# A two-layer gated cross-attention block on one NeuronCore: the softmax sums of half the heads of layer 1 move to ScalarE

## The chip, the core and the metric

The kernel runs on one core of one Trainium2 chip. A core has TensorE (matmuls, transposes), VectorE, ScalarE, GpSimd and SyncE, each with its own queue that it works off in order; they wait for each other by semaphores. The metric is the device time of one execution in microseconds; before the change it is 2202.97 us, the median of three runs (2202.91 to 2205.18).

## What is computed

The reference is a decoder block of two layers for 8 samples. Each layer adds a cross-attention over a context and a feed-forward net to x, both behind a tanh gate. Cut to what matters here (layer 1 is the `L0` part):

```python
x = x + tanh(g_xattn[0]) * L0_xattn(layernorm(x), ctx, ctx, Wq, Wk, Wv, Wo)   # 16 heads of 32
x = x + tanh(g_ffn[0])   * L0_ffn(layernorm(x), w1, conv_w, conv_b, w2)       # ternary weights, depthwise conv
x = x + tanh(g_xattn[1]) * L1_xattn(layernorm(x), ctx, mask, Wq, Wkv, Wo)     # 8 heads of 64, mask
x = x + tanh(g_ffn[1])   * L1_ffn(layernorm(x), w_gate, w_up, w_down)         # blockwise fp4
# L0_xattn, per sample and head:
scores = q @ k.T / sqrt(32)                 # 224 x 750
attn = softmax(scores, axis=-1)
out = (attn @ v) ... @ Wo.T
```

x is 8 x 224 x 512, the context 8 x 750 x 512, all in float32.

## The kernel before

The program is unrolled. One loop in `run` goes over 16 attentions: n = 0 to 7 are the samples of layer 1 (`attention16`), 8 to 15 those of layer 2 (`attention8`); afterwards `ffn1` does the second feed-forward net. Other work is cut into small pieces, Python generators that yield an estimate of the TensorE time and the VectorE time of the piece. The attention routines put such pieces between their own instructions: `fill(us, queues)` takes pieces until their TensorE time reaches `us`, `pace(us, beside)` takes pieces until VectorE is thought to be `us` behind, and `finish` takes all. The order that results stands in each engine's queue.

For a sample n of layer 1 the pieces are: `early` (the output projections of sample n - 1, L383; the second product of the feed-forward net of sample n - 2, L929; the values of sample n, L359), `late` (`keys_queries` of sample n + 1: keys L298, queries L327, transposes of the normed x, L185) and `beside` (`ffn0` of sample n - 1: the product with w1, L822, then hp L830 on VectorE, y L834 on ScalarE, the taps L846 on VectorE, tanh L876 on ScalarE, the gate L858; in sample 0 the ternary quantization of both feed-forward weights, L715 to L731). What a product leaves in PSUM is copied out by ScalarE: kT (L307), v (L368), xnT and xqT (L186), bc (L204). These copies share two banks, tag `m`, and one bank, tag `t`.

`attention16` has two halves. The 512 columns are 4 groups g of 4 heads; queries are in 2 tiles of 112, keys in 2 chunks of 375 for the scores and in 6 tiles of 125 for the weights.

- Maxima: 16 slots (g, i, c). Four score matmuls (L466), one for each head, write a PSUM tile `quad` of four banks; VectorE takes the maximum over the chunk for all four heads (L473). Then comes fill. The maxima of all groups are joined (L485), split into three bf16 parts, and transposed.
- Weights: 12 steps, three for each group. For two key tiles TensorE puts minus the maximum (L434, bf16) and then the transposed scores (L443) into `quad`; ScalarE takes the exponential of all four heads at once (L510); fill and pace follow; then the products of the weights with v and with ones (both L521) add up in the bank `pa`, for which each head uses 32 columns of the array. The products with ones give the softmax sum in all 32 rows of the head. After the third step VectorE takes the reciprocal of the sums (L530) and multiplies (L531).

`quad` is allocated once (bufs=1): the next scores or weights wait until VectorE or ScalarE is done with it.

At the end of layer 2 the first two blocks of the last feed-forward net are already begun (`ffn1_head`); the hidden values of block 0 are quantized (`quantized`, in pieces of 512 columns and three parts) before `ffn1` starts, and `ffn1` then works block by block (L1076, L1108), with the load of w_down (`wd`) at its start.

## Time and profile before

| what | before |
|---|---|
| median of three runs | 2202.97 us |
| the profiled execution | 2205.97 us, span 2204.2 us |
| TensorE busy | 2139.1 us (97%) |
| VectorE busy | 1390.8 us (63%) |
| ScalarE busy | 698.1 us (32%) |
| samples 0 to 7 of layer 1 | 31.6 to 1018.4 us |
| one of them (sample 4) | 124.58 us, of which the maxima to the first weights 59.8 |
| products with v, L521 | 1536 records, 93.3 us |
| products with ones, L521 | 1536 records, 91.0 us |

The span is from the first to the last instruction of the profiled execution. A float32 matmul has two records in the trace. Matmuls on different rows or columns of the array run at once, so the busy time of such a group is far below its count times the mean of one.

### The profile page before, as it was taken

To read this page: it belongs to the slowest core of one execution; us is meant where nothing else is said; L and a number is where in the kernel's file an instruction comes from. 1 tells how busy PE (TensorE), PEld (TensorE's weight loads), DVE (VectorE), ACT (ScalarE), POOL (GpSimd) and SP (SyncE) were. 2 spreads that over 40 slices of the span, in tenths; PEclk is the share of its full clock that TensorE was granted. 3 is DMA by queue.
4 is the path that set the end of the run, shared out by engine and by line. 5 is a ranking of instruction groups with operands and counts; after the bars stand their busy time and mean duration, and the time that the engine had idled before them with its cause. 6 is when DMAs were issued, how large, how long until landed. Compare 5 with 4: busy or idle time off the path is not lost.

```text
span 2204.2 us, 33275 instructions
## 1 busy us (share of the span) xinstructions
PE 2139.1 (97%) x14094; PEld 1239.6 (56%) x14094; DVE 1390.8 (63%) x2611; ACT 698.1 (32%) x1180; POOL 131.4 (6%) x145
## 2 busy tenths in 40 slices
PE   9999999999999999999999999999999998999999
PEld 5544536455554646455555665656656565655555
DVE  3786777676776777675366485755523357666665
ACT  1222415152432515152443353443434231111111
POOL 0000000000000000000000110101100001111111
PEclk9999999999999999999999999999999999999999
DMA  6210010100001010211002112022210011000000
GB/s 221 72 34 29 1 45 2 32 15 18 29 12 35 2 45 2 70 34 37 29 19 66 51 49 64 28 71 57 60 38 11 14 40 51 10 19 19 20 5 20
DMA packets 50213, 81.31 MB, mean 37 GB/s; under 512 B 3344, under 2 KB 29712, under 8 KB 49936
## 3 DMA queue, kind: packets, MB, share of 16 engines
q1 hardware_dynamic: 50064, 79.18, 11.4%
q8 instruction: 111, 1.82, 0.3%
q14 instruction: 38, 0.31, 0.0%
HBM read 65.28 MB, written 13.89 MB: 36 GB/s over the span
## 4 chain that ended last, share of the span: by engine, by line
PE 86%; DVE 10%; ACT 2%; issue 1%; DMA 1%; SPq 0%; POOL 0%; ACTq 0%; DVEq 0%; POOLq 0%
PE ps_m L359 16%; PE ps_m L298 11%; PE ps_big L1076 10%; PE ps_m L1108 6%; PE ps_pa L521 6%; PE ps_quad L466 5%; PE ps_m L383 5%; PE ps_m L327 4%; PE ps_half L618 4%; PE ps_half L678 4%; PE ps_pa L581 3%; PE ps_quad L443 3%; PE ps_t L822 2%; PE ps_m L1076 2%; PE ps_t L929 1%; PE ps_quad L434 1%
## 5 line engine op out<-in xcount | busy, mean ns | idle before, releaser
L298 PE MATMUL ps_m<-cx,wk 128*128 128x375 f32 x1024 | 364.4, 488 | 2.4 <-ACT kT L307 1.2
L359 PE MATMUL ps_m<-wv,cx 128*125 128x512 f32 x768 | 355.2, 603 | 0.0
L473 DVE TENSOR_REDUCE part<-ps_quad 112x4 f32<-112x1500 f32 x128 | 220.1, 1720 | 125.3 <-PE ps_quad L466 125.2
L298 PEld LDWEIGHTS ps_m<-cx,wk 128*128 128x128 f32 x1024 | 181.7, 191 | 104.0 <-issue 20.2
L359 PEld LDWEIGHTS ps_m<-wv,cx 128*125 128x125 f32 x768 | 136.0, 187 | 174.6 <-issue 162.7
L510 ACT ACTIVATE p<-ps_quad 125x1792 f32<-125x1792 f32 x96 | 159.8, 1664 | 204.1 <-PE ps_quad L443 204.1
L635 DVE CUSTOM_DVE_ANT_0 ps_half<-ps_half,mbias 112x750 f32<-112x750 f32 x128 | 121.1, 946 | 163.4 <-PE ps_half L618 162.9
L368 ACT COPY v<-ps_m 125x512 f32<-125x512 f32 x96 | 56.3, 586 | 487.4 <-PE ps_m L359 486.9
L1108 PE MATMUL ps_m<-wd,hqT 128*128 128x512 f32 x308 | 136.6, 592 | 0.0
L656 ACT ACTIVATE p<-ps_half,nm 112x750 f32<-112x750 f32 x128 | 113.3, 890 | 57.8 <-DVE nm L647 57.5
L383 PE MATMUL ps_m<-wo,aT 128*112 128x512 f32 x256 | 120.8, 602 | 1.1 <-DVE worth L758 1.1
L466 PE MATMUL ps_quad<-kT,qT 32*112 32x375 f32 x1024 | 115.2, 519 | 6.0 <-DVE part L473 6.0
L846 DVE SCALAR_TENSOR_TENSOR y<-hp,cw,y 128x224 f32<-128x224 f32 x256 | 109.6, 449 | 4.5
L1076 PE MATMUL ps_big<-wg,xqT 128*128 128x352 f32 x352 | 111.3, 459 | 0.0
L1076 PE MATMUL ps_big<-wu,xqT 128*128 128x352 f32 x352 | 111.3, 459 | 0.0
L327 PE MATMUL ps_m<-xnT,wq 128*128 128x224 f32 x512 | 109.7, 361 | 0.6 <-ACT xnT L186 0.6
L521 PE MATMUL ps_pa<-p,v 125*32 125x224 f32 x1536 | 93.3, 361 | 14.8 <-ACT p L510 14.8
L678 PEld LDWEIGHTS ps_half<-ident,p 112*125 112x125 f32 x768 | 93.2, 188 | 19.1 <-issue 7.6
L683 ACT COPY p<-ps_half 125x672 f32<-125x672 f32 x128 | 86.3, 723 | 43.4 <-PE ps_half L678 42.3
L327 PEld LDWEIGHTS ps_m<-xnT,wq 128*128 128x128 f32 x512 | 94.9, 192 | 8.9 <-issue 4.2
L678 PE MATMUL ps_half<-ident,p 112*125 112x112 f32 x768 | 95.8, 273 | 2.5 <-ACT p L656 2.5
L618 PE MATMUL ps_half<-kT,qT 64*112 64x375 f32 x512 | 97.5, 498 | 0.0
(207 smaller groups left out, 2829.0 us busy)
## 6 DMA issues: line engine op xcount, KB each, us to landing
cx<-in_ctx SPq DMA_DIRECT2D x32, 750.0 KB, 4.3
wst<-in_w SPq DMA_DIRECT2D x16, 512.0 KB, 8.2
x<-in_x SPq DMA_DIRECT2D x8, 448.0 KB, 6.2
mid<-x SPq DMA_DIRECT2D x8, 448.0 KB, 3.1
x<-mid SPq DMA_DIRECT2D x8, 448.0 KB, 3.6
last<-x SPq DMA_DIRECT2D x8, 448.0 KB, 3.1
out<-yout SPq DMA_DIRECT2D x14, 256.0 KB, 2.0
wraw<-in_w_gate SPq DMA_DIRECT2D x11, 256.0 KB, 2.7
```

The source lines that it names most:

```text
L298: nc.tensor.matmul(pk, lhsT=self.w["wk"][:, k, g * 128 : (g + 1) * 128], rhs=job["cx"][c][:, k, :], start=k == 0, stop=k == KC - 1,)
L327: nc.tensor.matmul(pq[:, g - g0, :], lhsT=self.w["wq"][:, k, g * 128 : (g + 1) * 128], rhs=xnT[:, k, :], start=k == 0, stop=k == KC - 1,)
L359: nc.tensor.matmul(pv, lhsT=job["cx"][c][:, k, at : at + CP], rhs=self.w["wv"][:, k, :], start=k == 0, stop=k == KC - 1,)
L383: nc.tensor.matmul(po, lhsT=aT[:, g, i * TP : (i + 1) * TP], rhs=self.w["wo"][:, g, :], start=g == 0, stop=g == KC - 1,)
L466: nc.tensor.matmul(sc[:, h, :MH], lhsT=qT[r, g, i * TP : (i + 1) * TP], rhs=kT[g][r, c * MH : (c + 1) * MH], start=True, stop=True,)
L473: nc.vector.tensor_reduce(part[:, i, g, :, c], sc[:, :, :MH], AX.X, ALU.max)
L510: nc.scalar.activation(p, pw[:, :, : 2 * S], AF.Exp)
L521: nc.tensor.matmul(pa[r, which, :], lhsT=self.ones[:CP, r] if which else job["v"][j][:, col : col + 32], rhs=p[:, h, (j - j0) * S : (j - j ...
L618: nc.tensor.matmul(sc[h][:, c, :MH], lhsT=qT[r, g, i * TP : (i + 1) * TP], rhs=kT[g][r, c * MH : (c + 1) * MH], start=True, stop=True,)
L678: nc.tensor.transpose(pt[:, j // half, j % half * TP : (j % half + 1) * TP], p[:, h, j * CP : (j + 1) * CP], self.ident[:TP, :TP],)
L1076: nc.tensor.matmul(ps[:, :CW], lhsT=xqT[:, k, :], rhs=wt[:, k, c0 : c0 + CW], start=k == 0, stop=k == KC - 1,)
L1108: nc.tensor.matmul(po, lhsT=hqT[:, k, :], rhs=wd[:, k, :], start=k == 0, stop=k == NC1 - 1)
```

## The change

1. In the maxima half the scores go into two PSUM tiles `pair` of two heads (two banks each, bufs=2) in place of one `quad`, with one reduction for each; the maxima are kept negated. The weights use the same two tiles, with one exponential for each.
2. For groups 2 and 3, ScalarE also takes the exponential of the scores in the maxima half, with the negated maximum of the chunk as its bias, and adds it up (`accum_out`): 32 instructions of 112 x 375 a sample. What is written is not used; only the sums are. `divisors` later scales them by exp(chunk maximum - maximum), adds the two chunks, takes the reciprocal, and spreads it over the 32 rows of each head by two transposes and two bf16 products (`stat_inv`, `spread_q`).
3. The products with ones are made for groups 0 and 1 only.
4. The products of a step come behind the next step's scores, and those of the last step behind the first scores of the next sample (`rest`).
5. The times of `fill` and `pace` change: 2.0 in the slots of groups 0 and 1, about 3.9 in those of groups 2 and 3, where `beside` pieces are taken as well; 1.2 or 2.0 in the weights.
6. The transposes of the queries use a bank `m` from sample 1 on (before: from sample 10), and the pieces of the queries come in the middle of a key group.
7. What is left of the quantization of block 0's hidden values goes into `ffn1` (`left`).

The diff, cut to its core:

```diff
@@ queries, keys_queries
-            self.transposed(xnT, xn, i, "m" if n > B + 1 else "t")
+            self.transposed(xnT, xn, i, "m" if n else "t")
...
-                yield from self.keys(n, c, g)
-                if (c, g) in ((0, 0), (0, 1), (0, 3), (1, 0), (1, 1)):
-                    yield next(q)
+                for k, cost in enumerate(self.keys(n, c, g)):
+                    yield cost
+                    if k == 1 and (c, g) in ((0, 0), (0, 1), (0, 3), (1, 0), (1, 1)):
+                        yield next(q)
@@ attention16, maxima
-                    sc = self.ps("quad", [TP, 4, 512])
+                    sc = [self.ps("pair", [TP, 2, 512]) for _ in range(2)]
...
-                    nc.vector.tensor_reduce(part[:, i, g, :, c], sc[:, :, :MH], AX.X, ALU.max)
+                    for k in range(2):
+                        nc.vector.tensor_reduce(
+                            part[:, c, i, g, 2 * k : 2 * k + 2],
+                            sc[k][:, :, :MH], AX.X, ALU.max, negate=True,
+                        )
+                    if (g, i, c) == (0, 0, 0):
+                        self.finish([before])
                     self.behind = 0
...
+                    if g < 2:
+                        self.fill(3.4 if n and (g, i, c) == (0, 0, 0) else 2.0, early, late)
+                        continue
...
+                    for h in range(4):
+                        nc.scalar.activation(
+                            shown[:TP, h, :MH],
+                            sc[h // 2][:, h % 2, :MH],
+                            AF.Exp,
+                            bias=part[:, c, i, g, h : h + 1],
+                            accum_out=sums[:, c, i, g - 2, h : h + 1],
+                        )
+                    if (g, i, c) == (KC - 1, NT - 1, 1):
+                        self.fill(3.9, early, late)
+                        continue
+                    self.pace(0.1, beside)
+                    self.fill(1.9, early, late)
+                    self.pace(0.1, beside)
+                    self.fill(2.0 + max(self.behind - 2.4, 0), early, late)
...
-        self.fill(3.3, early, late)
+        self.pace(0.1, beside)
+        self.fill(2.9, early, late)
@@ attention16, weights
+        def divisors():
+            less = pool.tile([TP, 2, NT, 2, 4], F32, name="less")
+            for c in range(2):
+                nc.vector.tensor_tensor(
+                    less[:, c], val[:, :, 2:4, :], part[:, c, :, 2:4, :], ALU.subtract
+                )
+            nc.scalar.activation(less, less, AF.Exp)
+            yield
+            nc.vector.tensor_tensor(sums, sums, less, ALU.mult)
+            total = pool.tile([TP, NT, 2, 4], F32, name="total0")
+            nc.vector.tensor_tensor(total, sums[:, 0], sums[:, 1], ALU.add)
+            nc.vector.reciprocal(total, total)
+            transposed = self.stat_rows(self.stat_inv, total.rearrange("p t g h -> p t h g"))
...
+            iT = transposed()
...
+            nc.scalar.copy(across, pi)
+            yield across
...
+        def products(g, j0, p):
...
+            for which in range(2 if g < 2 else 1):
...
+        for step in range(KC * NKT // 2):
+            g, j0 = divmod(2 * step, NKT)
+            pw = [self.ps("pair", [CP, 2, 512]) for _ in range(2)]
...
+            for k in range(2):
+                nc.scalar.activation(p[:, 2 * k : 2 * k + 2, :], pw[k][:, :, : 2 * S], AF.Exp)
+            self.behind = max(self.behind - 4.1, 0)
+            if last:
+                products(*last)
+            last = g, j0, p
+            if step in (1, 3, 4, 5):
+                banks["across"] = next(more)
...
+            self.pace(3.0, beside)
+            self.fill(1.2 if g < 2 else 2.0, late)
@@ ffn1, run
+        first = left(h[0])
...
+                if i in (2, 3, 7, 8, 11, 13, 16, 18, 19):
+                    next(first, None)
...
-        self.psum_pool(banks, quad=1)
+        self.psum_pool(banks, pair=2)
...
-        self.finish(beside)
+        while beside and self.head["ready"] is None:
+            self.piece([beside])
         self.finish([rest, self.project_out(2 * B - 1)])
```

More of the change, by code (lines that the diff above doesn't have):

```diff
@@ L107, in setup @@
         self.spread_r = c.tile([128, 2, 128], BF16, name="spread")
+        self.spread_q = c.tile([128, 2, 128], BF16, name="spread_q")
         for g in range(KC):
@@ L112, in setup @@
             nc.vector.tensor_copy(self.pick[:, g, :], one.to_broadcast([128, CP]))
+            if g < 2:
+                own = c.tile([128, 4], F32, name="own4", bufs=2)
+                nc.vector.tensor_reduce(own, rows[:, :, 3 * g : 3 * g + 3], AX.X, ALU.add)
+                nc.vector.tensor_copy(
+                    self.spread_q[:, g, :].rearrange("p (h r) -> p h r", h=4),
+                    own.unsqueeze(2).to_broadcast([128, 4, 32]),
+                )
         for k in range(2):
@@ L124, in setup @@
         ]
-        for st in self.stat[0] + self.stat[1]:
+        self.stat_inv = c.tile([TP, NT, 128], BF16, name="stat_inv")
+        for st in self.stat[0] + self.stat[1] + [self.stat_inv]:
             nc.gpsimd.memset(st, 0.0)
@@ L449, in weights_minus_max, with attention16 @@
                 )
-    def attention16(self, n, early, late, beside):
+    def attention16(self, n, before, early, late, beside):
         nc, pool, job = self.nc, self.att, self.jobs[n]
@@ L457, in attention16 @@
         rows = [slice(h * 32, (h + 1) * 32) for h in range(4)]
-        part = pool.tile([TP, NT, KC, 4, 2], F32, name="part")
+        part = pool.tile([TP, 2, NT, KC, 4], F32, name="part")
+        sums = pool.tile([TP, 2, NT, 2, 4], F32, name="sums")
         for g in range(KC):
@@ L463, in attention16 @@
                 for c in range(2):
-                    sc = self.ps("quad", [TP, 4, 512])
+                    sc = [self.ps("pair", [TP, 2, 512]) for _ in range(2)]
                     for h, r in enumerate(rows):
                         nc.tensor.matmul(
-                            sc[:, h, :MH],
+                            sc[h // 2][:, h % 2, :MH],
                             lhsT=qT[r, g, i * TP : (i + 1) * TP],
@@ L472, in attention16 @@
                         )
-                    nc.vector.tensor_reduce(part[:, i, g, :, c], sc[:, :, :MH], AX.X, ALU.max)
-                    self.behind = 0
-                    if n and g > 1 and (i, c) in ((0, 1), (1, 1)):
-                        self.pace(0.1, beside)
-                        self.fill(3.7 if self.behind > 0.5 else 1.72, early, late)
-                    else:
-                        self.fill(2.9 if n and (g, i, c) == (0, 0, 0) else 1.72, early, late)
-                        if self.behind > 0.5:
-                            self.fill(0.86, early)
@@ L484, in attention16 @@
-        val = pool.tile([TP, NT, KC, 4], F32, name="val")
-        nc.vector.tensor_reduce(
-            val.rearrange("p t g h -> p (t g h)"),
-            part.rearrange("p t g h c -> p (t g h) c"),
-            AX.X,
-            ALU.max,
-            negate=True,
-        )
+                    for k in range(2):
+                        nc.vector.tensor_reduce(
+                            part[:, c, i, g, 2 * k : 2 * k + 2],
+                            sc[k][:, :, :MH],
+                            AX.X,
+                            ALU.max,
+                            negate=True,
+                        )
@@ new lines, in attention16 @@
+                    if (g, i, c) == (0, 0, 0):
+                        self.finish([before])
+                    self.behind = 0
+                    if g < 2:
+                        self.fill(3.4 if n and (g, i, c) == (0, 0, 0) else 2.0, early, late)
+                        continue
+                    if (g, i, c) == (2, 0, 0):
+                        shown = pool.tile([CP, 4, 2 * S], F32, name="p", bufs=2)
+                    for h in range(4):
+                        nc.scalar.activation(
+                            shown[:TP, h, :MH],
+                            sc[h // 2][:, h % 2, :MH],
+                            AF.Exp,
+                            bias=part[:, c, i, g, h : h + 1],
+                            accum_out=sums[:, c, i, g - 2, h : h + 1],
+                        )
@@ L492, in attention16 @@
+                    if (g, i, c) == (KC - 1, NT - 1, 1):
[5 more added lines that the diff above has]
+                    self.fill(2.0 + max(self.behind - 2.4, 0), early, late)
+        val = pool.tile([TP, NT, KC, 4], F32, name="val")
+        nc.vector.tensor_tensor(val, part[:, 0], part[:, 1], ALU.min)
         transposed = self.stat_rows(self.stat[0][n % 2], val.rearrange("p t g h -> p t h g"))
-        self.fill(3.3, early, late)
+        self.pace(0.1, beside)
@@ L496, in attention16 @@
         self.fill(0.7, late)
-        self.behind = 0
-        aT = job["aT"] = pool.tile([128, KC, S], F32, name="aT")
-        for g in range(KC):
-            pa = self.ps("pa", [128, 2, S])
-            for j0 in range(0, NKT, 2):
-                pw = self.ps("quad", [CP, 4, 512])
-                k = kT[g][:, j0 * CP : (j0 + 2) * CP]
-                self.weights_minus_max(
-                    [(pw[:, h, : 2 * S], r, g, qT[:, g, :], k) for h, r in enumerate(rows)],
-                    self.pick, sT, True,
-                )
-                p = pool.tile([CP, 4, 2 * S], F32, name="p", bufs=2)
-                nc.scalar.activation(p, pw[:, :, : 2 * S], AF.Exp)
-                self.behind = max(self.behind - 5.8, 0)
-                self.pace(1.5, beside)
-                self.fill(2.05 - self.ahead(4.0 if j0 + 2 < NKT else 0.5, beside), late)
-                self.pace(4.0 if j0 + 2 < NKT else 0.5, beside)
-                self.owed = 0
-                for which in range(2):
-                    for j in (j0, j0 + 1):
-                        for h, r in enumerate(rows):
-                            col = g * 128 + h * 32
-                            nc.tensor.matmul(
-                                pa[r, which, :],
-                                lhsT=self.ones[:CP, r] if which else job["v"][j][:, col : col + 32],
-                                rhs=p[:, h, (j - j0) * S : (j - j0 + 1) * S],
-                                start=j == 0 and which == 0,
-                                stop=j == NKT - 1 and which == 1,
-                            )
-            inv = pool.tile([128, 2, S], F32, name="inv")
-            nc.vector.reciprocal(inv[:, 0, :], pa[:, 1, :])
-            nc.vector.tensor_tensor(aT[:, g, :], pa[:, 0, :], inv[:, 0, :], ALU.mult)
-            self.behind += 2.0
@@ new lines, in attention16 @@
+        self.behind = max(self.behind - 3.0, 0)
+        def divisors():
[3 more added lines that the diff above has]
+                    less[:, c], val[:, :, 2:4, :], part[:, c, :, 2:4, :], ALU.subtract
+                )
+            nc.scalar.activation(less, less, AF.Exp)
[5 more added lines that the diff above has]
+            transposed = self.stat_rows(self.stat_inv, total.rearrange("p t g h -> p t h g"))
+            self.behind += 2.0
+            yield
+            iT = transposed()
+            yield
+            pi = self.ps("t", [128, 2, S])
+            for k in range(2):
+                nc.tensor.matmul(
+                    pi[:, k, :], lhsT=self.spread_q[:, k, :], rhs=iT, start=True, stop=True
+                )
+            across = pool.tile([128, 2, S], F32, name="inv")
+            nc.scalar.copy(across, pi)
+            yield across
@@ new lines, in attention16 @@
+        aT = job["aT"] = pool.tile([128, KC, S], F32, name="aT")
+        more, banks = divisors(), {}
+        def products(g, j0, p):
+            if j0 == 0:
+                banks["pa"] = self.ps("pa", [128, 2, S])
+            pa = banks["pa"]
+            for which in range(2 if g < 2 else 1):
+                for j in (j0, j0 + 1):
+                    for h, r in enumerate(rows):
+                        col = g * 128 + h * 32
+                        nc.tensor.matmul(
+                            pa[r, which, :],
+                            lhsT=self.ones[:CP, r] if which else job["v"][j][:, col : col + 32],
+                            rhs=p[:, h, (j - j0) * S : (j - j0 + 1) * S],
+                            start=j == 0 and which == 0,
+                            stop=j == NKT - 1 and (which == 1 or g > 1),
+                        )
+            if j0 + 2 < NKT:
+                return
+            if g < 2:
+                inv = pool.tile([128, S], F32, name="inv16")
+                nc.vector.reciprocal(inv, pa[:, 1, :])
+                self.behind += 2.0
+            else:
+                inv = banks["across"][:, g - 2, :]
+                self.behind += 0.4
+            nc.vector.tensor_tensor(aT[:, g, :], pa[:, 0, :], inv, ALU.mult)
@@ new lines, in attention16 @@
+        last = None
+        for step in range(KC * NKT // 2):
+            g, j0 = divmod(2 * step, NKT)
+            pw = [self.ps("pair", [CP, 2, 512]) for _ in range(2)]
+            k = kT[g][:, j0 * CP : (j0 + 2) * CP]
+            self.weights_minus_max(
+                [(pw[h // 2][:, h % 2, : 2 * S], r, g, qT[:, g, :], k) for h, r in enumerate(rows)],
+                self.pick, sT, True,
+            )
+            p = pool.tile([CP, 4, 2 * S], F32, name="p", bufs=2)
+            for k in range(2):
+                nc.scalar.activation(p[:, 2 * k : 2 * k + 2, :], pw[k][:, :, : 2 * S], AF.Exp)
[5 more added lines that the diff above has]
+                banks["across"] = next(more)
+                if step > 3:
+                    self.fill(0.6, late)
+            self.pace(3.0, beside)
+            self.fill(1.2 if g < 2 else 2.0, late)
@@ L533, in attention16, with rest @@
         self.finish(late)
+        def rest():
+            products(*last)
+            yield 1.5, 2.0
+        return rest()
     def load_masks(self, b):
@@ L1153, in ffn1_head, with quantized @@
             at += width
-        def quantized(h):
+        h["ready"] = 0
+        def quantized(values):
             for c0 in range(0, HID1, D):
-                part = h[:, c0 : min(c0 + D, HID1)]
-                yield from self.fp4_steps(work, part, part, part.shape[1])
+                c1 = min(c0 + D, HID1)
+                part = values[:, c0:c1]
+                for k, cost in enumerate(self.fp4_steps(work, part, part, c1 - c0)):
+                    h["ready"] = c1 if k == 2 else None
+                    yield cost
         other = other.rearrange("p k m -> p (k m)")[:, :D].rearrange("p (k t) -> p k t", k=KC)
@@ L1186, in quantized, with left @@
                 yield from self.fp4_steps(pool, h[:, c0 : c0 + QW], h[:, c0 : c0 + QW], QW, 2)
+        def left(h):
+            for c0 in range(self.head["ready"], HID1, D):
+                part = h[:, c0 : min(c0 + D, HID1)]
+                yield from self.fp4_steps(pool, part, part, part.shape[1], 2)
         def banks():
@@ L1297, in last_weights @@
             )
+        rest = iter(())
         for n in range(2 * B):
@@ L1327, in run @@
                     early.append(self.project_out(n - 1))
-                self.attention16(n, early + [self.values(n)], late, beside)
+                rest = self.attention16(n, rest, early + [self.values(n)], late, beside)
                 self.finish(beside)
                 continue
-            values, ends = self.values(n), rest if n > B else iter(())
+            values, ends = self.values(n), rest
             def mixed(values=values, ends=ends):
```

## The prediction

> **What bounds the kernel now.** I read the page first, then the groups by line, then two timelines and a table of windows of one sample of the first layer (sample 4, 520.03 to 644.61 us; from sample 2 on they repeat within 0.3 us).

> ```profile
> PE 2139.1 (97%) x14094; PEld 1239.6 (56%) x14094; DVE 1390.8 (63%) x2611; ACT 698.1 (32%) x1180; POOL 131.4 (6%) x145
> ...
> DVE  3786777676776777675366485755523357666665
> ACT  1222415152432515152443353443434231111111
> ...
> PEclk9999999999999999999999999999999999999999
> ```

> TensorE is busy nearly all the time at full clock; ScalarE does a third of that. So a matmul taken away counts in full, unless TensorE then waits.

> ```profile
> 520.03:579.82 59.79, 59.41 (x265) 24.59 (x261) 42.84 (x59) 6.34 (x12) 1.38 (x2) 1.00 0.14 42
> 579.82:644.61 64.79, 61.82 (x777) 40.92 (x777) 44.73 (x82) 35.70 (x47) 0.00 (x0) 1.00 0.01 2
> ```

> These are the two halves of sample 4, maxima and then weights: length, then busy time of PE, PEld, DVE, ACT and POOL. In the maxima half ScalarE works 6.34 of 59.79 us. That is the room the change uses.

> ```profile
> 554.21 0.90 PE L466 MATMUL ps_quad<-kT,qT 32*112 32x375 f32 x8
> 554.31 0.59 ACT L368 COPY v<-ps_m 125x512 f32<-125x512 f32 x1 [3.87 <-PE ps_m L359]
> 555.03 1.98 PE L359 MATMUL ps_m<-wv,cx 128*125 128x512 f32 x4
> 555.17 1.72 DVE L473 TENSOR_REDUCE part<-ps_quad 112x4 f32<-112x1500 f32 x1 [0.92 <-PE ps_quad L466]
> 556.95 0.90 PE L466 MATMUL ps_quad<-kT,qT 32*112 32x375 f32 x8
> ...
> 641.24 1.66 ACT L510 ACTIVATE p<-ps_quad 125x1792 f32<-125x1792 f32 x1 [3.49 <-PE ps_quad L443]
> 642.80 0.47 ACT L307 COPY kT<-ps_m 128x375 f32<-128x375 f32 x1
> 642.96 0.96 PE L521 MATMUL ps_pa<-p,v 125*32 125x224 f32 x16 [1.03 <-ACT p L510]
> ```

> The first five are one score slot: scores at 554.21, the copy of an earlier v, two matmuls of other work, the reduce ending at 556.89, the next scores 0.05 us later. Such a slot lasts 2.74 us and TensorE loses nothing. The last three are a step that ran out of other work: its products wait for the exponential. From starts of successive matmuls I find only 3.0 us of waiting in the sample: 1.10 there, 1.28 before the query transposes (they share the bank of the feed-forward product), 0.45 at the last scores, 0.19 elsewhere. The other 121.6 us are matmul work.

> **What is removed and added on TensorE.** For groups 2 and 3 the 48 matmuls with ones go, two trace records each. In an undisturbed step four heads together take 0.189 us a pass (600.97 to 601.16), so the four passes of a step (two key tiles, two records each) are 4 x 0.189 = 0.757 us, and six steps 4.54 us. Added per sample are two small transposes and two bf16 products of the inverse sums (0.13 us each in L422 and L599 by their starts), about 0.5. The transposes' 1.28 goes as they move to the other bank; the products move behind the next scores, so the 1.10 goes too. If nothing else waited, a sample would take 124.58 - 4.54 - 3.0 + 0.5 = 117.5 us.

> **What is added on VectorE and ScalarE.** One reduce of 1500 becomes two of 750. L473 takes 1.72 us, successive starts 1.64; so one of 750 is 0.94, and the pair 1.80. The new exponentials have no row of 375 with a sum; the nearest is this.

> ```profile
> L656 ACT ACTIVATE p<-ps_half,nm 112x750 f32<-112x750 f32 x128 | 113.3, 890 | 57.8 <-DVE nm L647 57.5
> L656 ACT ACTIVATION_READ_ACCUMULATOR p<-ps_half,nm 112x1 f32 x128 | 25.9, 203 | 0.0
> L307 ACT COPY kT<-ps_m 128x375 f32<-128x375 f32 x128 | 60.1, 469 | 80.9 <-PE ps_m L298 80.3
> ```

> Two of them back to back start 0.872 us apart, the reading of the sum included. Less 375 elements at 0.83 ns (slope between L368 and L307) that is 0.56 for one of 375. The bounds are 0.50 (the sum's reading wholly hidden) and 0.77 (nothing overlaps); I take 0.56, for ScalarE overlaps in the row too. Four a slot are 2.25 us, eight slots 18 us a sample. Counted as load that is nothing: the maxima half then has 24 us on ScalarE in some 60.

> **Where occupancy misleads.** The row at 554.31 is a copy of v that starts 0.04 us after its matmuls end, because nothing stands ahead of it in ScalarE's queue. [...] I go by the row, which speaks of order. In the changed order every copy that empties the two work banks (v, kT, xnT, xqT) of a late slot stands behind that slot's four exponentials. Counted from the slot's first score, the scores are ready at 0.97, the first maximum at 1.91, the second at 2.77, the exponentials run from 1.96 to 4.2. So nothing else leaves ScalarE before 4.2, and TensorE, which runs some 5 us of work a slot, meets three places that need an earlier copy. I walked slots 8 to 15 of the changed order by these durations.

> Slot 11: the diagonals' product (L201) writes the bank that xqT has to leave. TensorE arrives at 2.97 (scores 0.93, four transposes 0.2, two values 1.8), xqT is copied by 4.88. Wait 1.9 us.

> Slot 14: VectorE still holds the norm of the next x from slot 13. After reduces, hp and taps it is at 4.95; statistics, GpSimd's power and xn took 3.17 us in sample 1 of the trace (193.39 to 196.56). So slot 14's reduces start at 3.05 instead of 0.97 and its exponentials end at 6.29. Tanh 0.46, two y of 0.47, then the kT copy of the key group that ended early in the slot: done at 8.2. TensorE wants that bank at 5.05. Wait 3.15. Behind it lie the next scores, so VectorE and ScalarE start the next slot late as well.

> Slot 15: xnT's copy stands behind its exponentials, done at 4.8; the next key group wants the bank at 2.75. Wait 2.05, and 0.15 for a later kT.

> The pair of tiles is no double buffer: a slot or step takes both. In slots 3, 5 and 6 the second reduce ends 0.1 later than the old one did: 0.3. In the weights two exponentials of 896 (0.80 apart, 0.92 long, against 1.66 for one) end at 2.96 from a step's start, so a step lasts at least 3.0. With full cover nothing shows, steps of 4 to 5 us being the rule; but since the score slots now take more of the keys and values, three have only 2 us (step 0, which has no products yet, and 10 and 11): 0.95 each, 2.85.

> Sum: 117.5 + 1.9 + 3.15 + 2.2 + 0.3 + 2.85 = 127.9 against 124.58, or +3.3 a sample, +20 for samples 2 to 7, whose order is the same.

> **The first two samples.** In sample 0 VectorE quantizes the first feed-forward weights (16 sums of 1.15, 16 triples of 2.1 us, 52 in all) and is the late engine. It starts on them in slot 8, one a slot, but the maxima end 17 us later than before, and only 8 us are done by then: its end moves from 146 to about 152 us. TensorE waits for it in products and in the sum of pieces (5.5 us, against 4.4 before), and as the last steps have no other work, six wait for exponentials. With 2 us of late copies sample 0 ends near 145.5 (143.7 before): +2. Sample 1 then waits 6.5 us in its first slot for the last group's division, behind those triples (1.2 before); its copies cost about 7, its uncovered steps 5; against 9.5 of waits and 4.0 of matmuls that go: +5.

> **The moved edits.** The end of the quantization of the first h now goes into the last stage.

> ```profile
> 1826.20 4.48 PE L1076 MATMUL ps_big<-wg,wq 128*128 128x352 f32 x7 [6.15 <-DVE gth L1088]
> ...
> 1824.62 0.69 DVE L1051 BATCH_NORM_STATS2 st<-xf 128x6 f32<-128x512 f32 x1 [12.32 <-DMA xf<-last]
> ```

> TensorE's 6 us there are VectorE waiting for the load xf, which follows the 10.9 us load of wd in SP's queue (1811.93 to 1822.82). wd waited for GpSimd's last product of h; now it waits for the last output projection (done about 1810.7), so it starts 1.2 us sooner; but a first piece of h (1.2 us) stands ahead of gth on VectorE. I cost it at 0, with bounds of -4 (the load gone from the path) and +2 (VectorE's 4 us of extra work not covered in that block). SP's order is otherwise the same; only the x of sample 1 now follows the eight loads of the first feed-forward weights (landed by 37.3 us) and is used after 70: 0. The finer interleaving of queries and keys in layer 2, and its bank, hides behind 1.0 us of such waits there: 0, at most 1 either way. The new constants cost about 1 us of VectorE before 18 us, under loads: 0.

> Sum: +20 + 2 + 5 + 0 = +27 us on a profiled execution of 2205.97 us (span 2204.2 and 1.8 around it), which lies 3.0 above the median of 2202.97. I take the difference over to the median: 2230 us.

> **The rivals.** First, faster: the copies come in time. It needs the three waits of slots 11, 14 and 15 to shrink from 7.1 to under 3.8 us a sample. For it: each is a difference of two times of 3 to 8 us, and an exponential of 0.50 and an earlier norm would take 3 us away. Against it: the order on ScalarE is fixed and the 4.2 us come from rows. With none of these waits a sample takes 120.6, -4.0, so -24 in six; with samples 0 and 1 at +3 together: 2182 us. Chance 0.25.

> Second, slower still: an exponential with its sum costs 0.77, as if the 203 ns were exposed. Then a slot's ScalarE ends 0.84 later; three waits of slots 11 to 15 and one more grow by that, 3.4 a sample, 27 in eight: 2257. Chance 0.15.

> Third, no visible change: half of the waits are absorbed by the neighbours, 2203 within 4 us. Chance 0.06. That the ones do not shorten TensorE, as they share the array with other columns, is unlikely, for their starts take 0.87 us of each step.

> My own case, 2212 to 2245, has 0.54.

> **The numbers.** 2230 us; slower by over 0.2% (4.4 us, what the spread of 2.3 us over three runs lets a measurement tell) 0.69, within it 0.06, faster 0.25. The range 2179 to 2250 takes in the middle of the faster case and part of the second rival; the slower case alone would be 2212 to 2247.

> **What would show it.** Right: in slots 8 to 15 of a sample PE waits of 2 to 3 us before the diagonals' product and before two key matmuls, released by ScalarE's copies; matmuls with ones halved to 768 records; the period of a sample near 128 us; ACT busy up by 150 us or more. Wrong: a period under 123 us with those waits under 1 us. A first slot of sample 1 without a wait on VectorE would make the +5 wrong, a wait for xf under 3 us the 0 at the end.

## The result: 2237.8 us, 1.5% slower, and the profile after

| | before | after |
|---|---|---|
| median of the runs | 2202.9 us | 2237.8 us (2235.3 to 2238.0) |
| ratio to before | | 1.0154 (95% interval 1.0136 to 1.0172) |
| profiled execution, its span | 2205.97 us, 2204.2 us | 2235.26 us, 2233.5 us |
| mean granted TensorE clock | 0.996 | 0.985 |

The profiled executions differ by 29.3 us, the medians by 34.9: the profiled execution of after lies below its median, that of before above. The working below is made between the profiled ones.

The page of after: busy time of the engines, then tenths of 40 slices.

```profile
PE 2134.3 (96%) x13358; PEld 1230.5 (55%) x13358; DVE 1385.7 (62%) x2823; ACT 850.7 (38%) x1812; POOL 131.0 (6%) x146
...
DVE  3686767766676676666384755856513457666674
ACT  1534636353553636356253343534434331111111
PEclk9989999999999999999999999999999999999999
```

ScalarE has 152.6 us more work and is still busy only 38% of the time. TensorE's busy time fell by 5 us, and the time rose by 29. No share of busy time in these rows shows why.

The two parts of sample 4 (length, then busy time of PE, PEld, DVE, ACT, POOL, then the clock):

```profile
532.47:614.38 81.91, 74.31 (x344) 33.71 (x348) 52.44 (x96) 31.30 (x92) 1.38 (x2) 0.98 0.10 31
614.38:661.17 46.79, 45.60 (x605) 30.12 (x599) 34.56 (x73) 29.74 (x47) 0.00 (x0) 1.00 0.01 2
```

The sample takes 128.70 us, against 124.58. In the maxima TensorE stands still for more than 7 of 81.91 us (before: 0.4 of 59.79), and the clock is below full. Three places make up most of that, here in the timeline of this sample; a bracket gives the idle time before a row and what ended it. First slot 11:

```profile
576.86 0.57 ACT L505 ACTIVATE p<-ps_pair,part 112x375 f32<-112x375 f32 x1 [1.57 <-DVE part L487]
...
577.42 0.56 ACT L505 ACTIVATE p<-ps_pair,part 112x375 f32<-112x375 f32 x1
...
578.52 0.58 ACT L505 ACTIVATE p<-ps_pair,part 112x375 f32<-112x375 f32 x1
...
579.07 0.54 ACT L195 COPY xqT<-ps_t 128x448 bf16<-128x448 bf16 x1
...
579.66 0.70 PE L210 MATMUL ps_t<-diag,ones 112*128 112x112 f32 x4 [1.91 <-ACT xqT L195]
```

The transposes of xqT had ended at 575.97. The copy that empties their bank starts 3.1 us later, when the four exponentials ahead of it are done, and the product with the diagonals waits 1.91 us for the bank. Then slots 14 and 15:

```profile
593.62 0.69 POOL L177 TENSOR_TENSOR rstd<-ve,neghalf 112x2 f32<-112x2 f32 x1 [27.95 <-DVE ve L175]
594.35 0.55 DVE L182 TENSOR_SCALAR xn<-x,mv,rstd 112x512 f32<-112x512 f32 x1 [0.87 <-POOL rstd L177]
594.81 1.78 DVE L487 TENSOR_REDUCE part<-ps_pair 112x2 f32<-112x750 f32 x2
...
597.49 0.57 ACT L505 ACTIVATE p<-ps_pair,part 112x375 f32<-112x375 f32 x1
...
598.51 1.04 ACT L918 ACTIVATE y<-hp,cb,cw 128x224 f32<-128x224 f32 x2
...
599.44 0.84 ACT L316 COPY kT<-ps_m 128x375 f32<-128x375 f32 x2
...
599.96 2.78 PE L307 MATMUL ps_m<-cx,wk 128*128 128x375 f32 x4 [3.42 <-ACT kT L316]
...
607.83 2.16 PE L307 MATMUL ps_m<-cx,wk 128*128 128x375 f32 x6 [2.07 <-ACT xnT L195]
```

The scores of slot 14 started at 591.59. Their reduces start 3.22 us later, behind the norm; exponentials, tanh and y follow, and only then come the two copies of kT that TensorE waits for. The four matmuls after that wait take 2.78 us where four such take 1.44 at 604.32, and the granted clock is 0.50 from 600.08 to 603.49 and 1.00 behind that. The table of windows (the clock is the third number from the end) shows this best in sample 3:

```profile
448.00:452.00 4.00, 3.09 (x8) 1.40 (x8) 0.00 (x0) 1.69 (x5) 0.00 (x0) 0.74 0.00 0
452.00:456.00 4.00, 4.00 (x21) 2.00 (x21) 2.15 (x3) 1.11 (x5) 0.00 (x0) 0.84 0.00 0
...
468.00:472.00 4.00, 1.15 (x2) 0.84 (x3) 2.17 (x6) 3.17 (x9) 0.00 (x0) 0.80 0.00 2
472.00:476.00 4.00, 4.00 (x16) 1.62 (x14) 0.71 (x1) 0.00 (x0) 0.00 (x0) 0.50 0.00 0
476.00:480.00 4.00, 2.91 (x9) 1.51 (x8) 2.77 (x11) 3.60 (x11) 0.00 (x0) 0.85 0.00 0
```

The second of these rows holds 4.00 us of busy TensorE at 0.84, so the number is not just idle time. The shares missing from 1.00 add up to 0.42 in the first two rows and 0.85 in the last three; times 4 us, and doubled, that is 3.4 and 6.8 us at half the clock. So TensorE pays for a wait twice here: the wait, and slower matmuls behind it. Samples 2 to 7 take 127.07, 130.74, 128.70, 130.75, 128.71 and 131.56 us.

### The profile page after: what moved, and what is told of

The parts are those of the page before. It is cut to its first block, busy times and chain, and to the rows that moved or that the text cites. A ratio compares the mean times of both kernels' runs of the same rounds, so it can differ in the third digit from the quotient of the medians.

```text
span 2233.5 us, 32844 instructions
## 1 busy us (share of the span) xinstructions
PE 2134.3 (96%) x13358; PEld 1230.5 (55%) x13358; DVE 1385.7 (62%) x2823; ACT 850.7 (38%) x1812; POOL 131.0 (6%) x146
## 3 DMA queue, kind: packets, MB, share of 16 engines
q8 instruction: 105, 1.72, 0.3%
## 4 chain that ended last, share of the span: by engine, by line
PE 84%; DVE 8%; ACT 6%; issue 1%; DMA 1%; POOL 0%; SPq 0%; ACTq 0%; POOLq 0%; DVEq 0%
PE ps_m L370 14%; PE ps_m L307 11%; PE ps_big L1160 10%; PE ps_m L1192 6%; PE ps_m L394 5%; PE ps_pair L479 5%; PE ps_m L336 4%; PE ps_pa L570 4%; PE ps_half L702 4%; PE ps_half L762 4%; PE ps_pa L665 3%; PE ps_pair L454 3%; ACT p L505 2%; DVE part L487 2%; PE ps_m L1160 2%; ACT p L600 1%
## 5 line engine op out<-in xcount | busy, mean ns | idle before, releaser
L307 PE MATMUL ps_m<-cx,wk 128*128 128x375 f32 x1024 | 371.0, 496 | 33.0 <-ACT kT L316 20.6
L487 DVE TENSOR_REDUCE part<-ps_pair 112x2 f32<-112x750 f32 x256 | 228.4, 934 | 191.8 <-PE ps_pair L479 190.9
L307 PEld LDWEIGHTS ps_m<-cx,wk 128*128 128x128 f32 x1024 | 186.5, 195 | 140.0 <-ACT kT L316 25.2
L505 ACT ACTIVATE p<-ps_pair,part 112x375 f32<-112x375 f32 x256 | 143.1, 571 | 161.0 <-DVE part L487 161.0
L600 ACT ACTIVATE p<-ps_pair 125x896 f32<-125x896 f32 x192 | 165.2, 912 | 100.4 <-PE ps_pair L454 100.3
L479 PE MATMUL ps_pair<-kT,qT 32*112 32x375 f32 x1024 | 125.8, 537 | 0.4
L1171 ACT ACTIVATE gth<-ps_big 128x352 f32<-128x352 f32 x48 | 22.2, 463 | 215.2 <-PE ps_big L1160 215.2
```

The lines of the kernel that those rows point to most:

```text
L307: nc.tensor.matmul(pk, lhsT=self.w["wk"][:, k, g * 128 : (g + 1) * 128], rhs=job["cx"][c][:, k, :], start=k == 0, stop=k == KC - 1,)
L479: nc.tensor.matmul(sc[h // 2][:, h % 2, :MH], lhsT=qT[r, g, i * TP : (i + 1) * TP], rhs=kT[g][r, c * MH : (c + 1) * MH], start=True, stop= ...
L487: nc.vector.tensor_reduce(part[:, c, i, g, 2 * k : 2 * k + 2], sc[k][:, :, :MH], AX.X, ALU.max, negate=True,)
L505: nc.scalar.activation(shown[:TP, h, :MH], sc[h // 2][:, h % 2, :MH], AF.Exp, bias=part[:, c, i, g, h : h + 1], accum_out=sums[:, c, i, g ...
L600: nc.scalar.activation(p[:, 2 * k : 2 * k + 2, :], pw[k][:, :, : 2 * S], AF.Exp)
```

## The experiments

Waits below are start-to-start distances less the usual one. They are up to 0.2 us longer than the brackets, and up to 0.5 us before a second group of four matmuls, which without a wait would start while the first group still runs (eight score matmuls in a row take 0.90 us, four take 0.89). The ratios are to before as timed together with the experiment. A "period" is the time of a sample from 3 to 6, which repeat.

**e1: without the exponentials.** The edit, with a constant put into `sums`:

```diff
-                    for h in range(4):
-                        nc.scalar.activation(shown[:TP, h, :MH], sc[h // 2][:, h % 2, :MH],
-                            AF.Exp, bias=part[...], accum_out=sums[...])
```

> The kernel after without the 256 exponentials in the maxima half (it leaves out the softmax sums of groups 2 and 3: a constant stands in their place); pairs, reduces, order and all else as after. Theory 1, the queue of ScalarE: the three waits of slots 11, 14 and 15 (2.04, 3.58 and 2.23 us in sample 4) go, and with them the stretches of lower granted clock; samples 2 to 7 take about 118.8 us in place of 128.7 to 130.7, sample 1 about 12 us less: 2162 us, and a mean clock of 0.995 or more. Rival, the two tiles and VectorE's norm ahead of the reduces: the wait of slot 14 stays at 2 us or more and the clock low; 2215 us or more.

Measured: 2184.4 us (ratio to before 0.9915, 0.9901 to 0.9930), period 122.79, clock 0.992. The exponentials cost 53.4 us, most of it as theory 1 has it: the waits of slots 11 and 15 are gone. But 2162 was too low. One long wait, of 2.23 us, stays in samples 2 to 7, at slot 14, and from sample 3 on 3.4 us of half clock follow it. In sample 4:

```profile
570.23 0.55 DVE L182 TENSOR_SCALAR xn<-x,mv,rstd 112x512 f32<-112x512 f32 x1 [0.87 <-POOL rstd L177]
570.69 1.78 DVE L488 TENSOR_REDUCE part<-ps_pair 112x2 f32<-112x750 f32 x2
...
573.04 1.04 ACT L908 ACTIVATE y<-hp,cb,cw 128x224 f32<-128x224 f32 x2 [4.89 <-DVE hp L904]
573.98 0.82 ACT L316 COPY kT<-ps_m 128x375 f32<-128x375 f32 x2
...
574.49 2.34 PE L307 MATMUL ps_m<-cx,wk 128*128 128x375 f32 x4 [2.07 <-ACT kT L316]
```

There is no exponential here, yet ScalarE stands for 4.89 us: its next instruction in order, y, needs hp, which VectorE makes behind the norm and the reduces. The copies of kT queue behind that y. So the rival was right on this one place, and theory 1 on the others. The edit that tells the norm from y is e5.

**e2: all sums on TensorE again.** e1's edit, `range(2)` for the products of all groups, the reciprocal from the bank, no `divisors`.

> The kernel after without any of its sums on ScalarE: products with ones for all four groups, reciprocal from the bank as before, no divisors. Pairs, late products, bank m, fill times as after. Theory: e1 plus 48 matmuls with ones (4.5 us) less the spreading of the inverse (0.5) a sample, 32 us in all: 2194 us, 0.4% faster than before, since what is left of the change only takes waits away. Rival, the products with ones run beside other columns and cost nothing: equal to e1 within 5 us. Rival, the pairs cost more than the late products bring: 2210 us or more.

Measured: 2207.8 us (1.0022, 1.0013 to 1.0032), period 125.9. Against e1, the ones of groups 2 and 3 less the spreading of the inverse are worth 23.4 us, where the theory had 32. They do not run for nothing beside other columns. I had expected what is left of the change to beat before; it is 0.2% slower. It has slot 14's wait of 2.23 in samples 2 to 7, and the half clock in five of the six.

**e3: exponentials two and two between the pieces.**

```diff
+                    self.fill(0.9, early, late)
+                    summed(0)
+                    self.fill(1.0, early, late)
+                    summed(1)
...
-                    self.fill(1.9, early, late)
```

> The kernel after with the four exponentials of a score slot issued as two and two between the pieces of other work (fill 0.9, two, fill 1.0, two, fill 2.0) in place of all four ahead of it. Theory 1, the order in ScalarE's queue: the copies of the first pieces stand ahead of the exponentials; the waits of slots 11 and 15 fall below 0.8 us, slot 14's to about 1.5, since its reduces still start late behind the norm; about 5.5 us of waits and 2 of low clock a sample go: 2190 us. Rival, VectorE's lateness and not the order: the wait of slot 14 stays above 3 us and the second pair, now later, holds up the next scores: 2230 us or more.

Measured: 2194.1 us (0.9960, 0.9945 to 0.9974), period 123.47. The work is that of after to the instruction, only the order differs, and 43.7 us go: the order in ScalarE's queue is the larger part of the cost. The waits of slots 11 and 15 are gone, slot 14's key group still waits 1.26 us, and new short waits of scores for the exponentials appear (0.79, 0.69, 0.85). This is the first of them:

```profile
569.10 0.89 PE L479 MATMUL ps_pair<-kT,qT 32*112 32x375 f32 x4 [0.72 <-ACT p L507]
```

**e4: before, with the queries' edit alone.**

```diff
-            self.transposed(xnT, xn, i, "m" if n > B + 1 else "t")
+            self.transposed(xnT, xn, i, "m" if n else "t")
...
-                yield from self.keys(n, c, g)
-                if (c, g) in ((0, 0), (0, 1), (0, 3), (1, 0), (1, 1)):
-                    yield next(q)
+                for k, cost in enumerate(self.keys(n, c, g)):
+                    yield cost
+                    if k == 1 and (c, g) in ((0, 0), (0, 1), (0, 3), (1, 0), (1, 1)):
+                        yield next(q)
```

> The kernel before with one edit alone: the transposes of the queries in bank m from sample 1 on, and the pieces of the queries in the middle of a key group. Theory: the 1.28 us of waiting before these transposes goes in seven samples (9 us), and layer 2 gains the 4 us that it gained in the kernel after: 2190 us. Rival, the wait only moves to the two banks m: 2203 us, as before. In the first layer the prediction took 1.28 a sample for it, in the second 0.

Measured: 2178.7 us (0.9888, 0.9873 to 0.9903), 24 us gained by two small edits where I expected 13; period 122.13 against 124.58. After contains these edits too, so against e4 the rest of the change costs 59 us and not 35.

**e5: e2, the norm not ahead of the reduces.**

```diff
-                    if k == 1 and (c, g) in ((0, 0), (0, 1), (0, 3), (1, 0), (1, 1)):
+                    if k == 1 and (c, g) in ((0, 0), (0, 2), (0, 3), (1, 0), (1, 1)):
```

> e2 (sums on TensorE for all groups) with one more edit: the first half of the next sample's normed x is made one key group later, so that it stands behind the reduces of slot 14 and not ahead of them. Theory 2, VectorE's norm (0.87 us of waiting for GpSimd's power and 0.55 for xn ahead of the reduces, then hp, then y, then the copy of kT): the wait of 2.23 us in slot 14 falls to about 0.9, and the clock stays at 1.00 there, which was 0.60 for a window of 4 us; 3.0 us a sample, 21 in seven: 2187 us. Rival, the two y ahead of the copy are enough for the wait: it stays at 2 us or more, 2205 us or more.

Measured: 2191.2 us (0.9944, 0.9930 to 0.9959), period 122.87. The wait in slot 14 is 0.81 us, and samples 2 to 7 have no stretch of low clock. Moving one VectorE instruction of 0.55 us by one slot brings 16.7 us. y ahead of the copies is as it was, so the lateness came from the norm.

**e6: e3 with the same edit.**

> e3 (exponentials two and two between the pieces) with the same edit. Theory 2: slot 14's reduces, y and exponentials come about 1.1 us sooner, the wait of 1.26 us before the last key group goes: 1.0 us a sample, 2187 us. Rival, ScalarE is simply full in slots 12 to 15 (2.25 us of exponentials, 1.04 of y, 0.58 of tanh, 0.46 to 0.92 of kT in slots of some 5 us): the order of VectorE changes nothing, 2192 to 2194 us.

Measured: 2188.8 us (0.9935, 0.9920 to 0.9950), period 122.43. The wait before the last key group falls from 1.26 to 0.23 us. The scores' waits (0.78, 0.69, 0.85) stay.

**e7: feed-forward pieces in every second slot only.** `if c and not final` ahead of both calls of `pace` in the slots.

> e6, and pieces of the feed-forward net are taken in every second slot of groups 2 and 3 only (those with the second key chunk). Theory: ScalarE loses 1.6 us a slot in half of them, so the waits of e3 behind exponentials (0.79, 0.69, 0.85 and 1.26 us in sample 4) go, and the uncovered steps of 0.80 get cover: some 4 us a sample against e3, 2165 us. Rival, VectorE: four slots of 3 us more go into the weights half, where it is busy 36 of 48 us now; then TensorE waits for it there, 2195 us or more.

Measured: 2276.9 us (1.0336, 1.0319 to 1.0354), period 133.80: 112 us above my number, and 82 above where the rival began. The work that the slots leave is not done in time beside the weights. The timeline at the end of sample 3:

```profile
548.05 1.67 DVE L951 TENSOR_REDUCE hmx<-hs 128x224 f32<-128x896 f32 x1
550.29 0.65 PE L983 MATMUL ps_t<-ident,hmx 128*112 128x128 f32 x2 [7.56 <-DVE hmx L959]
```

TensorE waits 7.56 us for the maximum of the feed-forward values, which VectorE has ready only then. Whether VectorE could do this work earlier is open: it is busy 8.11 of the 12 us from 523 to 535, and a shorter `pace` in the weights was not tried.

**e8: before, the bank alone.** The first hunk of e4.

> The kernel before with the transposes of the queries in bank m from sample 1 on, and nothing else of e4 (the pieces of the queries stay between key groups). e4 brought 2.45 us a sample in samples 2 to 7, 5.5 in sample 1, and 5.4 in layer 2, where the bank was m already from its second sample on. Theory: the bank alone takes away only the 1.28 us before the transposes; 2194 us, and layer 2 as before; the rest of e4 comes from the place in the middle of a key group, where the copy of the bank has two matmuls more of cover. Rival: the bank is everything in layer 1; samples 2 to 7 at 122.1 us, 2184 us.

Measured: 2192.5 us (0.9953, 0.9936 to 0.9969), period 122.57, layer 2 as before. The bank brings 2.0 us in each of samples 2 to 7, more than the 1.28 that I had counted as waits; the place in the key group brings 0.4 more there, all of the gain in sample 1 (127.05 in before, 127.65 in e8, 121.56 in e4) and 1.0 in most samples of layer 2. The result lies between theory and rival, nearer the theory.

**e9: e6, sample 0's last division ahead of the quantization.**

```diff
+                if n == 0:
+                    self.finish([rest])
                 self.finish(beside)
```

> e6, and in sample 0 the last products and their division are issued before what is left of the quantization of weights on VectorE. Theory (the prediction's reason for sample 1): the 7.0 us that TensorE waits in the first slot of sample 1 are that division behind the quantization; it falls to about 3, for the first reduces still stand behind the triples; sample 1 takes 125.5 us in place of 129.5: 2185 us. Rival: the quantization delays the reduces as much as the division, 2189 us as e6.

Measured: 2186.9 us (0.9928, 0.9911 to 0.9943). Sample 1 falls from 129.46 to 126.24 us, and sample 0 grows from 111.39 to 113.39. The wait was where I said, but most of it only moves; the total is not told apart from e6.

**e10: y behind the exponentials.** e9, with `fill(0.9)`, two, `fill(1.0)`, two, and only then the feed-forward pieces; in sample 0 these also start in the slots of group 1.

> e9, and two changes of order: in the score slots of groups 2 and 3 the pieces of the feed-forward net come after all four exponentials (so that no y stands between the reduces and the exponentials), and in sample 0 the quantization begins in the slots of group 1. Theory: the waits of scores behind late exponentials (0.78, 0.69 and 0.85 us in sample 4 of e6) go by two thirds, 1.5 us a sample, and the late end of the quantization comes some 5 us sooner: 2172 us. Rival: ScalarE's load in these slots and not the place of y makes the exponentials late, and the copies of kT now stand behind y again: 2185 us or more.

Measured: 2171.1 us (0.9855, 0.9840 to 0.9869), period 121.15, sample 1 116.3 us. The scores' waits are gone and the work is the same, so they came from y ahead of the exponentials and not from the load. Of the long waits one of 1.43 us is left, at the product with the diagonals; the two uncovered steps of 0.80 stay.

**e11: that product in bank m.**

```diff
-        pb = self.ps("t", [128, S])
+        pb = self.ps("m", [128, S])
```

> e10 with the product with the diagonals (L201 of before) in a bank m and not in bank t, which xqT has to leave. Theory (the prediction's reason for slot 11): the wait of 1.43 us before that product in e10 is the copy of xqT behind the exponentials of the slot; it goes, 1.4 us a sample and 2.6 in sample 1: 2160 us. Rival: bank m is no freer there, for the copies of v stand behind the same exponentials: the wait moves to the next value, 2171 us.

Measured: 2160.4 us (0.9801, 0.9785 to 0.9818), period 119.61, of which 2.1 us are waits. It does all that the change set out to do, and beats before by 43 us and after by 77. Its page:

```profile
PE 2113.0 (98%) x13358; PEld 1226.1 (57%) x13358; DVE 1387.5 (64%) x2823; ACT 851.4 (39%) x1812; POOL 130.2 (6%) x146
```

TensorE has exactly as many instructions as in after, and ScalarE and VectorE the same busy time within 2 us.

Put in a row, by the medians: before to e4, -24.3 (the queries' edit); e4 to e2, +29.1 (pairs, late products and fill, 16.7 of which e5 takes back by one place); e2 to e1, -23.4 (the ones, less the spreading); e1 to after, +53.4 (the exponentials in ScalarE's queue). These sum to +34.8.

## Why the prediction was right

The forecast was 2230 us, with a range of 2179 to 2250, and slower as the likeliest sign; it came out at 2237.8. The mechanism is the one forecast: small copies behind the exponentials in ScalarE's queue. The closeness of the number is in part luck, as the sum at the end shows. The signs named for "right" are all there: the three waits, 768 records of ones, 152.6 us more on ScalarE, and periods of 127 to 131 us. By ScalarE's busy share alone (32% before) the exponentials would cost nothing, and the 120.6 us a sample of the faster rival would be left: 2182 us, 56 too low. The steps:

**The three waits of slots 11, 14 and 15.** 1.9, 3.15 and 2.05 us forecast; 1.91, 3.42 and 2.07 in the brackets of sample 4, released by the copies that were named. e1 and e3 show the exponentials ahead of the copies as the cause in slots 11 and 15. In slot 14 the norm has its part, as the prediction had it (reduces 3.05 us after the scores; measured 3.22). The wait of 3.58 us there falls to 2.23 without the exponentials (e1) and to 0.81 when the norm is later as well (e5): about 1.35 for the one, 1.42 for the other. The later norm alone, with the exponentials as they are in after, was not run.

**The exponential.** 0.56 us forecast; in the timeline they start 0.55 to 0.57 us apart. The group rows give an exponential 571 ns and the reading of its sum 203 ns, and the second overlaps the first:

```profile
L505 ACT ACTIVATE p<-ps_pair,part 112x375 f32<-112x375 f32 x256 | 143.1, 571 | 161.0 <-DVE part L487 161.0
L505 ACT ACTIVATION_READ_ACCUMULATOR p<-ps_pair,part 112x1 f32 x256 | 51.9, 203 | 0.0
```

The second rival (0.77) falls with this.

**The work that is left.** 117.5 us a sample before any new wait; sample 2, which has no low clock, takes 127.07 and waits 9.8, so 117.2. The two terms in it were not so well sized one by one: e2 against e1 gives some 3 us a sample for ones less spreading (4.0 forecast), e8 2.0 us for the bank (1.28).

**Uncovered steps.** Three of 0.95 forecast; two of 0.80 found in each of samples 2 to 7.

**What was missing: the clock.** No step had a price for half speed after a wait. Samples 3 to 6 have the matmuls of sample 2 in the same order, and sample 2 has no low clock (1.00 from 204.13 to 449.89 us), so the difference is the price: 130.74 less 127.07 is 3.7 us in samples 3 and 5, 128.70 less 127.07 is 1.6 in 4 and 6; sample 7, at 131.56, has the 3.7 too. That is some 14 us in samples 2 to 7. Without it six samples of 127.07 would have cost 15 us, where the waits were forecast at 20; with it they cost 29.9. The trace of before held the hint, in a row that the prediction shows: seven matmuls at 1826.20, behind the wait of 6.15 us, take 4.48 us, and the granted clock is 0.50 from 1824.10 to 1830.92. The next seven, at 1.00, take half of that:

```profile
1831.00 2.23 PE L1076 MATMUL ps_big<-wu,wq 128*128 128x352 f32 x7
```

**Sample 0 and 1.** +2 and +5 forecast. Sample 1 is +5.8, with 6.86 us in its first slot for the division behind the quantization (6.5 forecast). Sample 0 takes 112.19 us against 112.14 and starts 1.9 us sooner, so it ends 1.9 sooner, not 2 later: that step failed. The end of the quantization was right (151.8 us, 152 forecast), but TensorE waited less for it: 4.0 us in brackets where 5.5 were counted, and two steps wait 0.80 us for exponentials where six were. The two samples together cost 5.8 us, 7 forecast.

**Layer 2 and the last net.** 0 forecast, at most 1 for the queries' place. Layer 2 is 3.7 us shorter up to the last net. This is the place of the queries in a key group: six samples lose about 1.0 us each, the same in e4, and none in e8. (Sample 9 of after is 1.9 us longer and takes part of it back; it holds a stretch of half clock, 3.41 us from 1234.96.) The step failed on size: I counted long waits alone, while in e4 a sample of layer 2 (the one whose scores start at 1513.5 us in before) gets its 1.0 us from many small ones: 0.34 at the query transposes, 0.30 at the products with v, 0.25 at the transposes of the weights. The last net gains 0.8, and still waits for xf:

```profile
1852.97 0.69 DVE L1135 BATCH_NORM_STATS2 st<-xf 128x6 f32<-128x512 f32 x1 [11.55 <-DMA xf<-last]
...
1855.51 4.64 PE L1160 MATMUL ps_big<-wg,wq 128*128 128x352 f32 x8 [5.42 <-DVE gth L1172]
```

The sum by the profiled executions: -1.9 at the start, 0 and +5.8 for samples 0 and 1, +29.9, -3.7 and -0.8 make 29.3. The forecast's +27 was that close in part because an unforeseen loss (the clock, 14) met errors the other way: waits of samples 2 to 7 forecast 5 too high, 3.9 less than forecast for the start and sample 0, and 4.5 gained in layer 2 and the last net.

**The faster rival.** It needed the three waits to shrink below 3.8 us; they are 7.4. e11 shows that the case was real, at 2160 us, only not in this order of instructions.

## What to carry to other kernels

Before work is moved to an engine that is idle two thirds of the time, list what stands behind it in that engine's queue and who waits for that; the cost here was not the 153 us of added work but copies of half a microsecond that queued behind it. Put the new work behind the small copies that free banks (order alone was worth 43.7 us in e3), and keep instructions that wait for a third engine (a norm that waits for GpSimd) out of the way of reduces that TensorE needs (16.7 us in e5). A change in several parts is best undone part by part: a loss of 35 us held a gain of 24 from two small edits.

## What was not expected of the hardware

A wait of TensorE of 2 us can be followed by half clock, and the same wait can pass without. In e1 the wait of 2.23 us is followed by 3.4 us at half clock in each of samples 3 to 7; in sample 2 it is not, and neither is the 3.58 us of sample 2 in after. In e5 the same place waits 0.81 us, and no low clock follows.

```profile
325.87:329.29 3.42, 2.27 (x8) 1.04 (x6) 3.30 (x6) 0.52 (x2) 0.05 (x1) 1.00 0.00 0
329.29:332.70 3.41, 2.49 (x14) 1.17 (x15) 1.73 (x5) 1.24 (x4) 0.00 (x0) 1.00 0.00 0
...
448.77:452.18 3.41, 1.34 (x5) 0.56 (x4) 3.34 (x8) 1.76 (x4) 0.00 (x0) 1.00 0.00 0
452.18:455.59 3.41, 3.41 (x13) 1.01 (x11) 0.25 (x1) 0.00 (x0) 0.00 (x0) 0.50 0.00 0
```

In sample 2 the grid splits the wait between two stretches, busy for 2.27 and 2.49 us; in sample 3 the wait lies in one, busy for 1.34 us, and half clock follows. Over the 13 runs, half clock followed all 60 stretches of full clock in which TensorE was busy for less than 43%, 12 of 23 at 43 to 48%, 6 of 169 at 48 to 75%, and none of the 7949 above. Half clock ended after all 74 stretches that were busy for 96% or more, and after 4 of 48 that were less. The limits are not sharp in these records. The grid also fits how samples repeat: 122.79 us, the period of e1, is 36 stretches less 0.1 us, and two samples of after, 259.44 us, are 76, so the wait comes back to the same place on the grid.
